# Ten transposes of a pair moved from TensorE to 32x32 VectorE turns with DMA block moves, x loaded transposed as well, and s_dst broadcast by DMA

## The chip, the cores and the metric

The kernel runs on one core of one Trainium2 chip. The metric is device time of one execution in microseconds (us), median over several executions. TensorE is called PE here, its weight loads PEld, VectorE DVE, ScalarE ACT, GpSimd POOL, and SP is the engine whose queue issues the DMAs.

## The reference, cut to what matters

x is (64, 256, 128) in fp32: 64 batches of 256 nodes with 128 features; `adj` is 256x256. Four graph layers follow each other, each added to its input and normalized per row:

```python
x = _layernorm(x + L0(x, adj, ...))   # gated recurrent cell, five steps
x = _layernorm(x + L1(x, adj, ...))   # two weights, softmax of a fixed adjacency
x = _layernorm(x + L2(x, adj, ...))   # attention over nodes, then a small MLP
x = _layernorm(x + L3(x, adj, ...))   # Chebyshev, seven weights
```

The attention of L2 is where one part of the change lies:

```python
h = einsum('bmi,ih->bmh', x, Wp) + bp
s_src = einsum('bmh,h->bm', h, a_src)
s_dst = einsum('bmh,h->bm', h, a_dst)
scores = s_src[:, :, None] + s_dst[:, None, :]      # s_dst is needed along the free axis, on every row
scores = where(scores >= 0, scores, 0.2 * scores)
attn = softmax(where(A <= 0, min, scores)) * A
h_gat = einsum('bmn,bnh->bmh', attn, h)
```

## The kernel before

The kernel works on 32 pairs of batches; a tile of a pair is 128 partitions x 512 fp32 (four blocks of 128 columns). The operations of all pairs are put into one list by a planner in the kernel (`Schedule`): it knows for each operation its engine or engines and a duration, and for each engine how long its result takes to be seen by others (`SEEN`, 2.5 us for a DMA issued by SP). The list that comes out is emitted in the order of the planned starts. In the traces an engine takes its queue in the order of the built list: in the kernel after, all 3510 DVE records stand in that order, and so do, line by line, those of ACT and PE's matmuls.

```python
CLASSES = {"X": (512, 12), "A": (512, 34), "H": (516, 5), "B": (1024, 9), "S": (32, 64), "PS": (512, 8)}
SEEN = {"PE": 0.3, "ACT": 0.15, "DVE": 0.15, "POOL": 0.2, "SP": 2.5}
ABREAST = 4
...
    def transposes(i, x_like):
        t = Value("PS", name="ps")
        def fn():
            for c in range(4):
                nc.tensor.transpose(t.at(4, P)[:, c, :], x_like(i)[:, c, :], ident.ap)
        pe(0.46, fn, [i, ident], [t])
        return t

    def spread(i, right):                     # adjacency times a tile: the tile is the stationary operand
        ...
                    nc.tensor.matmul(t.at(2, N)[:, b, :], tokens(i)[:, 2 * b + j, :], right.ap[:, j, :], ...)

    def layer_norm(y, o):
        s, mv, rs = stats(y)                  # bn_stats on DVE, power -0.5 on POOL
        def fn():
            for c in range(4):
                nc.vector.tensor_scalar(tokens(o)[:, c, :], tokens(y)[:, c, :], mv()[:, c, 0:1], rs()[:, c:c + 1],
                                        op0=ALU.subtract, op1=ALU.mult)
        dve(1.4, fn, [y, s], [o])

    def layer2(x2):
        xT = to_sbuf(transposes(x2, tokens), "xT")
        ...                                   # h = x Wp + bp, with s_src as one more column
        sd, u, s = Value("PS", name="ps"), Value("B", name="u"), Value("S", name="nm")
        pe(mm(512), lambda: nc.tensor.matmul(sd.at(512), vdst.ap, xT.at(512), start=True, stop=True), [vdst, xT], [sd])
        for b in range(2):
            dve(0.68, lambda b=b: nc.vector.tensor_add(u.at(4, N)[:, 2 * b:2 * b + 2, :],
                    sd.at(512)[:, None, b * N:(b + 1) * N].to_broadcast([P, 2, N]), maskb.ap), [sd, maskb], [u])
        ...
```

`vdst` is a matrix whose columns are all Wp a_dst, so one matmul gives s_dst on every partition at once.

## Time and profile before

| | before |
|---|---|
| time, median of 3 | 1831.45 us (1829.76 to 1832.07) |
| PE busy, middle 1340 us | 1310 us |
| PE idle, summed over the table of waits | 81 us |

PE is what the time is made of: whatever takes a microsecond of PE work away may shorten the run, and whatever makes PE wait may lengthen it. The lines that carry this are in the prediction.

### The profile page before, as it was taken

The page shows a single profiled execution, that of the slowest core. Times are in us where ns is not written, and L with a number is a line of the kernel's source. Part 1 is how long each engine was busy: PE and PEld are TensorE (multiplying, and loading weights), DVE is VectorE, ACT ScalarE, POOL GpSimd, SP SyncE. Part 2 cuts the span into 40 slices and gives each one's busy share as a digit, 9 for nine tenths or more (in the row PEclk, how much of TensorE's full clock was granted, in tenths as well). Part 3 has the DMA queues.
Part 4 walks back from the last instruction along what each step waited for, and adds up shares of the span by engine and source line. Part 5 has one row for each costly group of instructions (what it writes and reads, how often), then busy time and mean ns, then how long its engine had stood idle before and what let it go on. Part 6 is the DMA issues. An engine that isn't in the chain of part 4 may idle for free. (4 is left out here: it accounts for less than half of the span.)

```text
span 1832.3 us, 22228 instructions
## 1 busy us (share of the span) xinstructions
PE 1741.1 (95%) x7856; PEld 1230.3 (67%) x7856; DVE 1194.5 (65%) x3536; ACT 793.5 (43%) x1586; POOL 438.8 (24%) x519
## 2 busy tenths in 40 slices
PE   8999999999999999999999999999999999998767
PEld 6567576767767667676776666666766667665566
DVE  5466666667767667667776577665667666665753
ACT  3444445444445454434444444444444444443322
POOL 0022212312231221222222212231123222111152
PEclk9999999999999999999999999999999999999778
DMA  4000000000000000000000000000000000000000
GB/s 119 1 1 12 12 12 1 12 12 13 7 12 7 18 6 7 12 13 11 8 13 12 13 12 1 12 12 7 7 0 7 6 7 7 6 1 6 1 1 24
DMA packets 35024, 20.50 MB, mean 11 GB/s; under 512 B 1248, under 2 KB 34528, under 8 KB 34912
## 3 DMA queue, kind: packets, MB, share of 16 engines
q1 hardware_dynamic: 34912, 19.08, 3.6%
q8 instruction: 61, 1.00, 0.2%
q14 instruction: 51, 0.42, 0.1%
HBM read 10.69 MB, written 8.39 MB: 10 GB/s over the span
## 5 line engine op out<-in xcount | busy, mean ns | idle before, releaser
L173 ACT COPY a<-ps 128x512 f32<-128x512 f32 (+1 forms) x532 | 278.5, 541 | 483.5 <-PE ps L400 286.0
L419 POOL TENSOR_SCALAR s<-s 128x4 f32<-128x4 f32 x160 | 49.5, 310 | 986.1 <-DVE s L416 986.1
L400 PE MATMUL ps<-aT,a 128*128 128x256 f32 x1024 | 242.8, 379 | 1.7 <-ACT a L173 1.6
L400 PEld LDWEIGHTS ps<-aT,a 128*128 128x128 f32 x1024 | 189.9, 190 | 49.5 <-issue 24.5
L422 POOL TENSOR_TENSOR s<-s,neg_half 128x4 f32<-128x4 f32 x192 | 200.4, 1044 | 15.9
L430 DVE TENSOR_SCALAR x<-a,s 128x128 f32<-128x128 f32 x384 | 120.9, 370 | 100.1 <-POOL s L422 99.9
L462 DVE TENSOR_TENSOR a<-a,a 128x512 f32<-128x512 f32 x160 | 121.0, 756 | 95.4 <-ACT a L460 95.2
L460 ACT ACTIVATE a<-ps,bzrh 128x512 f32<-128x512 f32 x160 | 109.9, 687 | 160.6 <-PE ps L458 160.5
L446 ACT ACTIVATE a<-ps,bzrh 128x512 f32<-128x512 f32 x160 | 109.4, 685 | 160.1 <-PE ps L443 156.8
L448 DVE SCALAR_TENSOR_TENSOR a<-a,a 128x512 f32<-128x512 f32 x160 | 120.9, 759 | 81.1 <-ACT a L446 80.5
L414 DVE BATCH_NORM_STATS2 s<-a 128x6 f32<-128x128 f32 x640 | 141.5, 279 | 47.9 <-ACT a L173 45.7
L450 PE MATMUL ps<-a,w 128*128 128x512 f32 x320 | 163.0, 600 | 7.2 <-ACT a L446 7.0
L458 PE MATMUL ps<-a,u5h 128*128 128x512 f32 x320 | 164.4, 595 | 4.9 <-DVE a L448 4.9
L443 PE MATMUL ps<-a,w 128*128 128x512 f32 x320 | 163.6, 593 | 1.8 <-ACT a L173 1.8
L457 PE MATMUL ps<-a,w 128*128 128x512 f32 x320 | 164.5, 596 | 0.0
L442 PE MATMUL ps<-a,W 128*128 128x512 f32 x320 | 163.9, 594 | 0.0
L481 PEld LDWEIGHTS ps<-W,a 128*128 128x128 f32 x1024 | 131.7, 196 | 36.6 <-issue 17.9
L481 PE MATMUL ps<-W,a 128*128 128x128 f32 x1024 | 135.6, 281 | 8.7 <-DVE a L488 4.4
L452 ACT ACTIVATE a<-ps,bzrh 128x512 f32<-128x512 f32 x160 | 110.0, 688 | 62.7 <-PE ps L450 61.3
L400 PE MATMUL ps<-aT,x 128*128 128x256 f32 x512 | 129.3, 391 | 8.1 <-DVE x L430 7.7
L463 DVE SCALAR_TENSOR_TENSOR a<-a,a 128x512 f32<-128x512 f32 x160 | 118.5, 745 | 16.3 <-ACT a L452 13.9
L382 PEld LDWEIGHTS ps<-ident,a 128*128 128x128 f32 x768 | 92.4, 142 | 53.3 <-issue 23.2
(140 smaller groups left out, 2645.6 us busy)
## 6 DMA issues: line engine op xcount, KB each, us to landing
x<-x_in SPq DMA_DIRECT2D x32, 256.0 KB, 2.8
y_out<-a SPq DMA_DIRECT2D x32, 256.0 KB, 2.3
W<-mats_in SPq DMA_DIRECT2D x1, 832.0 KB, 6.7
W<-mats_in SPq DMA_DIRECT2D x1, 512.0 KB, 3.7
rbc<-rows_in SPq DMA_DIRECT2D x1, 385.0 KB, 7.2
aT<-adjT_in SPq DMA_DIRECT2D x1, 256.0 KB, 4.7
a<-adj_in SPq DMA_DIRECT2D x1, 256.0 KB, 5.9
ccol<-cols_in SPq DMA_DIRECT2D x1, 6.0 KB, 3.5
```

Source lines behind the costliest of these rows:

```text
L173: S.add([("ACT", us_act, lambda: nc.scalar.copy(o(), i())), ("DVE", us_dve, lambda: nc.vector.tensor_copy(o(), i()))], r, w)
L400: nc.tensor.matmul(t.at(2, N)[:, b, :], tokens(i)[:, 2 * b + j, :], right.ap[:, j, :], start=(j == 0), stop=(j == 1))
L414: nc.vector.bn_stats(st.at(4, 6)[:, c, :], tokens(y)[:, c, :])
L422: pool(1.04, lambda: nc.gpsimd.tensor_tensor(rs(), rs(), neg_half.ap, op=ALU.pow), [s, neg_half], [s])
L430: nc.vector.tensor_scalar(tokens(o)[:, c, :], tokens(y)[:, c, :], mv()[:, c, 0:1], rs()[:, c:c + 1], op0=ALU.subtract, op1=ALU.mult)
L442: nc.tensor.matmul(t.at(512), mat("u3"), hT.at(512), start=True, stop=False)
L443: nc.tensor.matmul(t.at(512), w345.ap[:, 1, :], mT.at(512), start=False, stop=True)
L450: pe(mm(512), lambda t=t, mT=mT: nc.tensor.matmul(t.at(512), w345.ap[:, 0, :], mT.at(512), start=False, stop=True, skip_group_check=True), ...
L457: nc.tensor.matmul(t.at(512), w345.ap[:, 2, :], mT.at(512), start=True, stop=False)
L458: nc.tensor.matmul(t.at(512), u5h.ap, r.at(512), start=False, stop=True)
L462: dve(0.7, lambda hv=hv, hT=hT: nc.vector.tensor_sub(hv.at(512), hv.at(512), hT.at(512)), [hv, hT], [hv])
L481: nc.tensor.matmul(tokens(t)[:, c, :], i.at(4, P)[:, c, :], w(), start=(k == 0), stop=(k == len(lefts) - 1))
```

## The change

The intent is to take PE work away. (1) Ten of the twelve calls of `transposes` in a pair (four blocks each) become "turns"; two of the ten make up one tile of 1024 columns, so there are nine turns: DVE transposes each 32x32 block in place of its tile, one DMA stores the tile in DRAM, and four DMAs load it so that the blocks are where they belong. A turned tile is interleaved: the 128 columns of block t are every fourth column (every eighth in the 1024-wide tile, wT). (2) x is given a second time, transposed, so that layer 0 needs no transpose for its start. (3) s_dst comes as one more column of h; a DMA stores that column to DRAM ("the line") and a second one loads it onto all 128 partitions. (4) The normalization is split: DVE makes the product -mean*rstd, then ACT or DVE scales. In the attention of L2 the product with the adjacency moves in front of the turn, to POOL or DVE. (5) Buffers, `ABREAST` and the order of a few additions follow from that; the last three pairs keep their turns on PE.

```diff
+ABREAST = 2
+BY_PE = 3
+    def tile(self, t, n=512):
+        return self.ap[:, t:n:n // P] if self.moved else self.ap[:, t * P:(t + 1) * P]
 ...
+    def turn(i, name, o=None, n=512):
+        ...                                  # the last BY_PE pairs: transposes on PE, as before
+        st = Value(cls, name="turn")
+        dve(n / 512 * 0.62 + 0.06, lambda: nc.vector.transpose(st.at(n).rearrange("p (b l t) -> p t b l", b=4, l=32),
+                                                               i.at(n).rearrange("p (t b l) -> p t b l", b=4, l=32)), [i], [st])
+        d = Value("D", name="turn")
+        S.add([("SP", 0.45, lambda: nc.sync.dma_start(d.at(n), st.at(n)))], [st], [d])
+        def move():
+            for f in range(4):
+                nc.sync.dma_start(o.at(n)[32 * f:32 * f + 32].rearrange("r (b n) -> r b n", b=4),
+                                  d.at(n)[:, f * n // 4:(f + 1) * n // 4].rearrange("(b r) n -> r b n", b=4))
+        S.add([("SP", 1.8, move)], [d], [o])
+        o.moved = True
 ...
-                    nc.tensor.matmul(t.at(2, N)[:, b, :], tokens(i)[:, 2 * b + j, :], right.ap[:, j, :],
+                    nc.tensor.matmul(t.at(2, N)[:, b, :], i.tile(2 * b + j), right.ap[:, j, :],
 ...
+        nmr = lambda: s.at(32)[:, 12:16]
+        dve(0.16, lambda: nc.vector.scalar_tensor_tensor(nmr(), mv()[:, :, 0], -1.0, rs(), op0=ALU.mult, op1=ALU.mult), [s], [s])
+    def normalize(y, o, s, rs, nmr):
+        ...                                  # y * rs + nmr
+        S.add([("ACT", 1.85, by_act), ("DVE", 1.45, by_dve)], [y, s], [o])
 ...
-        pe(mm(512), lambda: nc.tensor.matmul(sd.at(512), vdst.ap, xT.at(512), start=True, stop=True), [vdst, xT], [sd])
+        line = lambda *ap: bass.AP(tensor=d.ap.tensor, offset=d.ap.offset, ap=ap)
+        S.add([("SP", 0.45, lambda: nc.sync.dma_start(line([1, P], [P, 4]), hs()[:, :, D + 1]))], [h], [d])
+        S.add([("SP", 0.45, lambda: nc.sync.dma_start(sd.at(512), line([0, P], [1, 512])))], [d], [sd])
```

(The same replacement of `transposes` by `turn` and of block indexing by `tile` is made in all layers; the cuts are marked by "...".)

## The prediction

> **What bounds the kernel now.** I read the head of the page and its 40 slices first, then the busy time by stretch, then TensorE's own timeline in the middle of the run, and last the groups of instructions and the DMA rows. The head and the slices:
>
> ```profile
> span 1832.3 us, 22228 instructions
> PE 1741.1 (95%) x7856; PEld 1230.3 (67%) x7856; DVE 1194.5 (65%) x3536; ACT 793.5 (43%) x1586; POOL 438.8 (24%) x519
> PE   8999999999999999999999999999999999998767
> PEclk9999999999999999999999999999999999999778
> ```
>
> TensorE is busy in nearly every slice until the last three, where its clock falls too. No other engine is above 65%. The table of stretches says how close to full it is:
>
> ```profile
> 0.00:60.00 60.00, 53.67 (x200) 35.18 (x201) 33.46 (x86) 21.76 (x36) 0.83 (x7) 1.00 0.32 91
> 60.00:1400.00 1340.00, 1310.30 (x5934) 920.44 (x5933) 897.58 (x2603) 603.20 (x1201) 326.30 (x380) 1.00 0.03 9
> 1700.00:1832.00 132.00, 91.45 (x482) 77.69 (x480) 73.06 (x295) 38.99 (x101) 40.62 (x52) 0.80 0.03 9
> ```
>
> In the long middle PE (first busy column) works 1310 of 1340 us. The tail of 132 us has only 91 us of PE work at a clock of 0.80. So this is a TensorE-bound kernel with a latency-bound tail. Matmul durations overlap, so I price PE by the distance between starts:
>
> ```profile
> 902.29 0.60 PE L382 MATMUL ps<-ident,x 128*128 128x128 f32 x4
> 902.73 1.89 PE L400 MATMUL ps<-aT,a 128*128 128x256 f32 x8
> 904.46 1.02 PE L457 MATMUL ps<-a,w 128*128 128x512 f32 x2
> 905.32 1.02 PE L458 MATMUL ps<-a,u5h 128*128 128x512 f32 x2
> 906.17 1.50 PE L481 MATMUL ps<-W,a 128*128 128x128 f32 x12
> 907.51 0.60 PE L382 MATMUL ps<-ident,a 128*128 128x128 f32 x4
> ```
>
> Four transposes take 0.44 us (0.11 each), eight 256-column records 1.73 us (0.216 each), two 512-column records 0.86 us (0.43 each), twelve 128-column records 1.34 us (0.112 each). An fp32 matmul shows as two records, a transpose as one. The groups that the change touches:
>
> ```profile
> L382 PE MATMUL ps<-ident,a 128*128 128x128 f32 x768 | 114.3, 277 | 13.8 <-DVE a L465 11.5 <-DVE a L430 2.3
> L382 PE MATMUL ps<-ident,x 128*128 128x128 f32 x512 | 77.5, 279 | 2.9 <-DVE x L430 2.9
> L284 PE MATMUL ps<-ident,b 128*128 128x128 f32 x256 | 37.2, 285 | 10.6 <-ACT b L529 10.6
> L510 PE MATMUL ps<-a,vdst 128*128 128x512 f32 x64 | 34.2, 616 | 0.0
> L173 ACT COPY a<-ps 128x512 f32<-128x512 f32 x418 | 236.0, 587 | 364.2 <-PE ps L400 286.0 <-PE ps L382 69.2 <-DVE a L564 3.0
> x<-x_in SPq DMA_DIRECT2D x32, 256.0 KB, 2.8
> y_out<-a SPq DMA_DIRECT2D x32, 256.0 KB, 2.3
> 178.00 0.39 SPq L602 DMA_DIRECT2D y_out<-a  x1
> ```
>
> [...] the trace's one undisturbed 512-column add from SBUF (line 305) took 692 ns, so I use it, as an estimate, for the block turns. [...] the two whole 256 KB trips in the trace take 2.3 us (store) and 2.8 us (load). [...]
>
> **The change part by part.** Counts come from the built instruction lists of both kernels.
>
> *PE, removed.* Transposes fall from 1544 to 256: 44 of the 48 of a pair in 29 of 32 pairs (the last three keep theirs, except the four of the first x), 29 x 44 + 3 x 4 = 1288. At 0.11 us that is 141.7 us. The 32 s_dst matmuls are 64 records at 0.43 = 27.5 us. Together 169 us, and all of it lies on the engine that sets the pace. Check of the whole: before, 1664 x 0.43 + 2832 x 0.216 + 1536 x 0.112 + 256 x 0.1125 + 1544 x 0.11 = 1698 us of PE pace; the other 134 us of the span are start, small gaps, tail and slow clock. After: 1529 us.
>
> *DVE.* Added: 232 turns of 512 columns x 0.69 + 29 turns of 1024 x 1.22 [...] = 195 us; 160 small scale products x 0.16 = 26 us. Removed: PSUM copies 62 to 15 (47 x 0.687 = 32 us); normalizations 640 to 292 because ACT may take them now (348 x 0.36 = 125 us); the products with aT 64 to 10 (54 x 0.684 = 37 us). Net +27: 1195 becomes about 1222 us, not the bound.
>
> *ACT.* Copies 418 to 270 (-148 x 0.587 = -87), normalizations 128 to 476 (+348 x 0.465 = +162): about 868 us. *POOL* gains 54 products of 128x512, 1.35 us each from its similar rows (1.30 to 1.44): +73, about 512 us. Neither binds.
>
> *SP and DMA.* 64 DMAs of the loop become about 1465: 261 stores to DRAM, 4 x 261 loads, 64 for s_dst, 96 for x, its transpose and y. At 0.39 us plus a gap of 0.07 between issues each takes 0.46, so 674 us: SP is some 40% occupied. Bytes: 29 x (8 x 0.5 + 1 MB) = 145 MB plus loads, about 95 GB/s, where the existing 19 MB took 3.6% of the 16 DMA engines. The 512-byte pieces of a turn are like those of an x load. Scaled by bytes, 28%, maybe 40% with the many small pieces: room enough.
>
> *Latency.* One turn now takes 0.69 (DVE) + 2.3 (store) + three further issues 1.4 + 2.3 to 2.8 (last load) = about 7 us, against 0.44 + 0.59 (transpose and ACT copy). That is +6 us for each of nine turns, and +4 for s_dst (2.3 + 2.8 against 0.86): nearly 60 us per pair. The first result left at 178 us, so a pair lives some 170 us and about 3.3 pairs overlap at 52 us of PE work each. After: 230 us and 47 us, five pairs. Twelve x tiles and 36 A tiles should allow that, so most of the latency hides behind other pairs. It comes out at the start and wherever the fixed order of an engine queue, above all the one SP queue, runs late; I charge 25 us more idle PE.
>
> *Sum.* 1529 + 134 + 25 = about 1690 us, if a weight load from a moved tile costs what a dense one costs.
>
> **Rivals.**
>
> *Strided weight loads.* A moved tile is read as every fourth fp32[...]. Such tiles are the stationary operand of 48 records of 256 columns and 32 of 128 columns per pair (wpx 8, the attention product 16, zT 8). [...] Against it: the changed kernel's scheduler prices these matmuls as before, in a kernel otherwise carefully priced.
>
> *DMA latency becomes the wait.* With one in-order issuer, each store must land before its four loads are issued; if turns of different pairs hardly overlapped, 9 x 4.5 us (store 2.3, issues 1.8, gaps) + s_dst 5 = 46 us per pair, which is just PE's 47. Then PE would wait everywhere and the time would be 1800 to 1900. For it: one queue. Against it: the built list interleaves stores of two or three pairs before loads.
>
> *VectorE becomes the bound.* If the turns' strided writes ran at half rate, +29 x (8 x 0.53 + 1.07) = 154 us: DVE 1376, still below 1690, but its queue would delay others: 1720 to 1750.
>
> *Tail.* The scheduler now ranks all but the last two pairs by age instead of the last four; the tail may grow by 10 to 20 us. Keeping the last pairs on PE speaks against more.
>
> **Range and chances.** I weigh the plain case (about 1690) at 0.5, half-rate weight loads (about 1780) at 0.33, stalls of DMA or DVE (1750 to 1900) at 0.17. The middle of that is 1712 us; eight times in ten between 1650 and 1800. Faster by over 2% means below 1795: 0.80; within 2%: 0.12; slower: 0.08.
>
> **What would show it.** Right: PE busy near 1560 us, above 90% of the middle slices, transposes 256, DVE near 1220, a store landing in about 2.3 us. Half-rate weight loads: weight-load records of moved tiles well above 190 ns and starts of the attention product 0.2 us apart instead of 0.112. DMA stalls: PE idle before the matmuls that read moved tiles, released by DMA, over 100 us in sum. DVE: turns well above 0.69 us, and PE waiting for DVE. The prediction is wrong if moved tiles are read slower than half rate, or if the SP queue runs so late that PE drops below 85% in the middle.

## More of the kernel before

The framework that builds the kernel can still order the emitted instructions a second time, which matters later (e16, e17).

One more group is needed later, for comparison: the weight loads of two matmuls whose stationary operand the change will lay out differently. The columns are line, engine, operation, tiles, shape and count, then the busy sum and mean ns of one, then idle time.

```profile
L400 PEld LDWEIGHTS ps<-aT,a 128*128 128x128 f32 x1024 | 189.9, 190 | 49.5 <-issue 24.5 <-ACT a L173 4.1 <-ACT a L460 0.5
...
L543 PEld LDWEIGHTS ps<-h,b 128*128 128x128 f32 x512 | 63.2, 195 | 8.6 <-issue 5.1 <-DVE b L535 2.2 <-DVE x L430 0.2
```

Both load 128x128 in about 0.19 us, beside running matmuls.

## The result, and the profile after

The changed kernel takes 2097.54 us (2096.17 to 2100.61, 4 runs) against 1831.03 us for the kernel before in the same rounds; the ratio is 1.1458, with a 95% interval of 1.1438 to 1.1478. It is correct and clearly slower. (All ratios here are the mean time of one kernel's fast runs over the mean of the other's fast runs of the same rounds, so they are not quite the ratio of the medians quoted.) The prediction was 1712 us, with 1800 as the upper end of its range.

The head of the page and the slices of PE and its clock, after:

```profile
span 2094.4 us, 22712 instructions
...
PE 1785.4 (85%) x6504; PEld 1273.9 (61%) x6504; DVE 1360.7 (65%) x3510; ACT 845.6 (40%) x1784; POOL 509.1 (24%) x573
...
PE   8998798888987889988788788987989888967846
...
PEclk9999999999998999999999899999999999978978
```

PE executes 1352 records fewer than before (6504 against 7856) and yet is busy 44 us longer, and in most slices it is busy for only seven or eight tenths. So two things happened: what is left on PE is slower, and PE waits. No other engine is near its limit. The summed idle time before PE's records rose from 81 to 301 us. The stretch in the middle says the same (PE is the first busy column, the clock and the DMA share are the two fractions near the end):

```profile
60.00:1400.00 1340.00, 1177.17 (x4147) 824.79 (x4146) 902.19 (x2197) 542.95 (x1112) 310.50 (x341) 0.95 0.37 98
```

Where before 1310 of these 1340 us were PE work, it is now 1177. The DMA engines are busy 0.37 of the time, so they are not full. How long the new DMAs take, from issue to landing in us (last column):

```profile
d<-a SPq DMA_DIRECT2D x232, 256.0 KB, 2.1
a<-d SPq DMA_DIRECT2D x928, 64.0 KB, 2.1
...
a<-d SPq DMA_DIRECT2D x32, 256.0 KB, 4.9
...
d<-h SPq DMA_DIRECT2D x32, 2.0 KB, 9.3
```

The first two rows are the turns, and they are as quick as I had assumed. The last two are the line: the store of 2 KB takes 9.3 us, over four times as long as the store of 256 KB, and its broadcast 4.9 us. Two waits answer to it (us in total, times, longest), one in the table of the engines' waits and one in that of the DMA queue:

```profile
DVE b L567 <- DMA a<-d: 171.3, 26, 14.2
```

```profile
SPq L565 <- DMA d<-h: 199.3, 28, 11.6
```

DVE stands for 171 us in sum at the addition that reads the line, up to 14.2 us at a time. One such place in the timeline:

```profile
893.60 0.76 DVE L559 TENSOR_TENSOR h<-ps,hbias 128x260 f32<-128x260 f32 x2
...
894.38 0.38 SPq L564 DMA_DIRECT2D d<-h  x1
...
904.19 0.34 SPq L565 DMA_DIRECT2D a<-d  x1
...
908.22 0.69 DVE L567 TENSOR_TENSOR b<-a,maskb 128x512 f32<-128x512 f32 x1 [8.93 <-DMA a<-d]
908.83 0.68 DVE L545 TENSOR_TENSOR a<-ps,a 128x512 f32<-128x512 f32 x1
...
909.57 1.11 PE L398 MATMUL ps<-ident,x 128*128 128x128 f32 x4 [4.48 <-DVE a L545]
...
910.47 1.92 PE L511 MATMUL ps<-a,w 128*128 128x512 f32 x2
...
912.18 1.91 PE L512 MATMUL ps<-a,u5h 128*128 128x512 f32 x2
```

The column of h is ready at 894.4; the store needs until 904.2, the load until 908.2. DVE idles 8.93 us at L567. L545, which has nothing to do with the line and belongs to another pair, stands behind it in DVE's queue, and PE waits 4.48 us for L545. Then PE's two-record matmul starts 1.71 us before the next (910.47 to 912.18), where before the change it was 0.86: after these 4.48 us of idle time it runs at half pace. The trace shows the clock granted to PE: it is 1.00 in the stretch from 893 to 906 us, 0.50 from 908.2 to 914 us, and 1.00 again from 915 us.

The other loss shows in the groups. These three answer to the two weight-load groups of before and to the estimate of 0.69 us for a turn:

```profile
L447 PEld LDWEIGHTS ps<-aT,a 128*128 128x128 f32 x1024 | 256.4, 315 | 65.8 <-issue 33.5 <-DMA a<-d 8.6 <-DVE s L463 5.4
...
L422 DVE STREAM_TRANSPOSE a<-a 128x512 f32<-128x512 f32 x174 | 190.8, 1107 | 9.3 <-ACT a L482 5.2 <-PE ps L637 1.4 <-PE ps L447 0.4
...
L598 PEld LDWEIGHTS ps<-h,b 128*128 128x128 f32 x512 | 122.0, 326 | 15.1 <-issue 11.5 <-ACT b L188 0.9 <-DMA t<-xT_in 0.2
```

A weight load from an interleaved tile takes 0.32 us on the mean instead of 0.19, the last pairs' dense ones included, and a turn of 512 columns takes 1.107 us.

### The profile page after: what moved, and what is told of

It reads as the page before. It is cut to its first block, busy times and chain, and to the rows that moved or that the text cites. A ratio compares the mean times of both kernels' runs of the same rounds, so it can differ in the third digit from the quotient of the medians.

```text
span 2094.4 us, 22712 instructions
## 1 busy us (share of the span) xinstructions
PE 1785.4 (85%) x6504; PEld 1273.9 (61%) x6504; DVE 1360.7 (65%) x3510; ACT 845.6 (40%) x1784; POOL 509.1 (24%) x573
## 2 busy tenths in 40 slices
DMA packets 253164, 189.50 MB, mean 90 GB/s; under 512 B 40048, under 2 KB 215152, under 8 KB 253040
## 5 line engine op out<-in xcount | busy, mean ns | idle before, releaser
L188 ACT COPY a<-ps 128x512 f32<-128x512 f32 (+1 forms) x379 | 194.5, 518 | 368.5 <-PE ps L447 214.3
L447 PEld LDWEIGHTS ps<-aT,a 128*128 128x128 f32 x1024 | 256.4, 315 | 65.8 <-issue 33.5
L447 PE MATMUL ps<-aT,a 128*128 128x256 f32 x1024 | 274.3, 410 | 17.4 <-DMA a<-d 16.7
L533 PEld LDWEIGHTS ps<-W,a 128*128 128x128 f32 x1024 | 159.8, 228 | 64.4 <-ACT a L188 21.0
L422 DVE STREAM_TRANSPOSE a<-a 128x512 f32<-128x512 f32 x174 | 190.8, 1107 | 9.3 <-ACT a L482 5.2
L533 PE MATMUL ps<-W,a 128*128 128x128 f32 x1024 | 166.4, 311 | 34.2 <-ACT a L188 10.9
L471 DVE SCALAR_TENSOR_TENSOR s<-s 128x4 f32<-128x4 f32 x192 | 45.3, 236 | 173.4 <-POOL s L469 173.0
L567 DVE TENSOR_TENSOR b<-a,maskb 128x512 f32<-128x512 f32 x64 | 43.0, 706 | 171.3 <-DMA a<-d 171.3
L512 PEld LDWEIGHTS ps<-a,u5h 128*128 128x128 f32 x320 | 60.7, 198 | 136.5 <-DVE a L502 77.2
L482 ACT ACTIVATE x<-a,s 128x128 f32<-128x128 f32 x212 | 90.5, 485 | 116.1 <-DVE s L471 116.0
```

The source lines that it names most:

```text
L188: S.add([("ACT", us_act, lambda: nc.scalar.copy(o(), i())), ("DVE", us_dve, lambda: nc.vector.tensor_copy(o(), i()))], r, w)
L422: dve(n / 512 * 0.62 + 0.06, lambda: nc.vector.transpose(st.at(n).rearrange("p (b l t) -> p t b l", b=4, l=32), i.at(n).rearrange("p (t b ...
L447: nc.tensor.matmul(t.at(2, N)[:, b, :], i.tile(2 * b + j), right.ap[:, j, :], start=(j == 0), stop=(j == 1))
L482: nc.scalar.activation(tokens(o)[:, c, :], tokens(y)[:, c, :], AF.Identity, bias=nmr()[:, c:c + 1], scale=rs()[:, c:c + 1])
L512: nc.tensor.matmul(t.at(512), u5h.ap, r.at(512), start=False, stop=True)
L533: nc.tensor.matmul(tokens(t)[:, c, :], i.tile(c), w(), start=(k == 0), stop=(k == len(lefts) - 1))
```

## The experiments

The first theory was: the line through DRAM costs most, because in-order queues stand behind it; the interleaving costs about 100 us; the turns' own trips are mostly hidden. The rivals: what PE waits for is the turns' trips through the one SP queue, or the interleaving is the main loss. The theory of the line had to be changed once on the way (e5, e16). "before" in the ratios is the kernel before in the same rounds, 1831 to 1832 us.

| label | what runs | us | ratio to before |
|---|---|---|---|
| (after) | the whole change | 2097.54 | 1.1458 |
| e1_sdst_pe | s_dst on PE | 1935.95 | 1.0573 |
| e2_dense_weights | moved tiles read dense (wrong results) | 2062.1 | 1.126 |
| e3_dense_turn_writes | turns written dense (wrong results) | 2047.57 | 1.1174 |
| e4_turns_by_pe | turns on PE | 2119.12 | 1.1573 |
| e5_line_planned | the plan knows the line's latency | 2090.53 | 1.1415 |
| e6_sdst_pe_dense_both | e1 with e2 and e3 (wrong results) | 1825.44 | 0.997 |
| e7_turns_sdst_by_pe | e1 with e4 | 1872.28 | 1.0225 |
| e8_turns_sdst_by_pe_ab4 | e7 with ABREAST = 4 | 1882.47 | 1.028 |
| e9_line_16B | the line stored in 16-byte pieces | 1989.62 | 1.0871 |
| e10_before_strided | kernel before, weights read interleaved (wrong results) | 1944.0 | 1.0613 |
| e11_before_xT | kernel before, x loaded transposed as well | 1829.92 | 0.9991 |
| e12_turns_sdst_norm_by_pe | e7, normalization as before | 1837.58 | 1.0029 |
| e13_turns_few | e12 with the turns of layers 0 and 3 | 1827.3 | 0.9975 |
| e14_turns_only_dense | e12 with all turns, dense (wrong results) | 1803.71 | 0.9847 |
| e15_turns_only | e12 with all turns | 1898.74 | 1.0366 |
| e16_line_planned_turns_by_pe | e4 with e5 | 2145.23 | 1.1715 |
| e17_line_planned_turns_by_pe_held | e16, built order held to the plan | 1778.29 | 0.9715 |
| e18_line_planned_held | e5, built order held to the plan | 1922.06 | 1.0499 |

"Wrong results": the data come out in the wrong order, while every instruction, its size and its waits stay.

**e1_sdst_pe: s_dst back on PE.**

```diff
-        S.add([("SP", 0.45, lambda: nc.sync.dma_start(line([1, P], [P, 4]), hs()[:, :, D + 1]))], [h], [d])
-        S.add([("SP", 0.45, lambda: nc.sync.dma_start(sd.at(512), line([0, P], [1, 512])))], [d], [sd])
+        def scores():
+            for c in range(4):
+                nc.tensor.matmul(sd.at(4, P)[:, c, :], vdst.ap, xT.tile(c), start=True, stop=True)
+        pe(mm(512), scores, [vdst, xT], [sd])
```

> Only the s_dst part undone: a TensorE matmul broadcasts s_dst again (four 128-column matmuls), the turns stay. Theory LINE (the 4-byte-piece store of s_dst takes 9.3 us, its load 4.9 us, the in-order SP and DVE queues stand behind it, and TensorE then restarts at half clock): DVE's 171 us of waiting on it go, the time falls by 170 us or more, to about 1900, although PE work grows by about 30 us. Theory WEIGHTS (slow loads of strided stationary tiles are nearly all of the loss): the time stays near 2080 to 2110. Theory TURN LATENCY (the trip of a turn through DRAM is what stalls PE): also near 2080.

Measured: 1935.95 us, 162 us below the kernel after. The line costs that much, although its removal gives PE work back. That work is itself slower than before, because the moving operand xT is interleaved here: the 256 records are 393 ns long on the mean, against 278 ns in e6, where xT is read dense, and they start 0.216 us apart on the mean instead of 0.114. That is some 26 us of PE work (256 x 0.102) which e1 and e15 have and the real change doesn't, since there s_dst is not PE's. The line is the largest single loss but not the whole of it.

**e2_dense_weights and e3_dense_turn_writes: the interleaving alone, at one end each.**

```diff
 e2: -        return self.ap[:, t:n:n // P] if self.moved else self.ap[:, t * P:(t + 1) * P]
     +        return self.ap[:, t * P:(t + 1) * P]
 e3: -  nc.vector.transpose(st.at(n).rearrange("p (b l t) -> p t b l", b=4, l=32), ...
     +  nc.vector.transpose(st.at(n).rearrange("p (b t l) -> p t b l", b=4, l=32), ...
```

> Wrong results on purpose: TensorE reads each moved tile as 128 neighbouring columns instead of every fourth; all else and the order of instructions are the same. WEIGHTS: from the records of the changed kernel, 29 pairs x (32 records x (0.230-0.112) + 48 x (0.247-0.216)) = 153 us of PE pace go; the time falls to about 1945. LINE or TURN LATENCY: PE has 15% idle and waits for others, so less than half of it shows, 2030 or more. Weight-load records of the attention product should fall from a mean of 326 ns to about 195.

> Wrong results on purpose: VectorE writes the turned blocks in runs of 32 neighbouring columns instead of every fourth; DMA and TensorE are unchanged. A turn of 512 columns should fall from 1107 to about 690 ns, 121 us of DVE work in all. If VectorE's work is on the path the time falls by 60 to 120 us, to about 2000; if it lies beside other work (DVE is 65% busy) by less than 40, to 2060 or more.

Measured: 2062.1 and 2047.57 us, 35 and 50 us below the kernel after. The mechanism shows in the records: with dense reads the weight loads of the attention product fall to 217 ns and PE's busy time from 1785 to 1695 us; with dense writes a turn takes 700 ns instead of 1107. But PE saved 90 us of busy time in e2 and only 35 us of the run: PE was waiting, and finished its work sooner only to wait longer (its summed idle time rises from 301 to 358 us). In e3 DVE saves 95 us and the run 50, which lies between the two forecasts: DVE's slow turns are partly on the path. In a kernel that stands still elsewhere, taking away one cost underrates it.

**e4_turns_by_pe and e7_turns_sdst_by_pe: no turns by DVE at all, with and without the line.**

```diff
-BY_PE = 3
+BY_PE = 32
```

> All ten turns of every pair on TensorE as in the last three pairs; s_dst still goes through DRAM, x still comes transposed. PE pace 1529 + 29 x 44 x 0.11 = 1669 us with no strided weights, no DVE turns and no DMA trips but that of s_dst. LINE: the stall of s_dst stays, and the time is 1900 to 2000, slower than the kernel before. WEIGHTS or TURN LATENCY: the time is near the kernel before less its saved transposes of x, about 1800 to 1830.

> Turns and s_dst on TensorE; left of the change are x loaded transposed, the normalization on either engine, the product with the adjacency before the transpose, the scheduler's two abreast. LINE: PE pace 1698 - 14 (transposes of x) = 1684 us, + 134 = about 1818, so some 300 us below the run with turns on TensorE and s_dst through DRAM, and a shade faster than before. If that run's loss came from the other small changes instead, it stays above 2000.

Measured: 2119.12 us with the line and 1872.28 without. Both forecasts for e4 missed: it is slower than either theory had it. With not one turn going through DRAM the kernel is no faster, which speaks against the turns' trips as what stalls the kernel after, and the line alone accounts for 247 us between the two. The comparison is not clean, since in e4 the wait at the line is longer than the 171.3 us of the kernel after:

```profile
DVE b L567 <- DMA a<-d: 257.7, 31, 18.5
```

But e7 is not back at 1832 us either, with turns and s_dst both on PE. Something else of the change costs about 40 us. (A more direct sign against the turns' trips: in the kernel after, PE's waits for the turns' loads sum to 37 us, where the prediction asked for over 100.)

**e8_turns_sdst_by_pe_ab4 and e12_turns_sdst_norm_by_pe: what is left in e7.** e8 sets `ABREAST = 4` as before; e12 gives the normalization back its old form (layer 2's first one, on ACT with the product, was so before):

```diff
     def layer_norm(y, o):
-        normalize(y, o, *stats(y))
+        s, mv, rs = stats(y)
+        dve(1.4, fn, [y, s], [o])            # tensor_scalar: subtract mean, multiply by rstd
```

> As the previous run but with the scheduler's last four pairs abreast again, as in the kernel before. If two abreast costs in the tail, 5 to 20 us faster than the previous run, about 1805; if not, the same within 5 us.

> Turns and s_dst on TensorE, and the normalization as in the kernel before (no scale product that sends the result from POOL through VectorE, only one engine allowed). If the way the normalization is split costs the 40 us that its parent lost against the kernel before: about 1825 to 1840. If the order of product and transpose, the tiles or the two abreast cost them: the same as the parent, 1872 within 8.

Measured: 1882.47 us, 10 us worse than e7, so ABREAST is not it; and 1837.58 us, 35 us better. The split normalization costs what was missing, with the order as built. Why it does is only argued. DVE waits for POOL's power about as long in both forms: 219.9 us in sum before its product in e7 (L474), 201.8 us before its normalizations and the one product that is left in e12. New in e7 is a further hop: where ACT scales, it waits for DVE's product, 130.8 us in sum against 71.4 us in e12. PE does not wait for that itself; what it waits for most in e7 is DVE's update in layer 0 (L522, 33.9 us), which may come late behind the products. No run takes the hop alone.

**e6_sdst_pe_dense_both: no line and no interleaving.** The edits of e1, e2 and e3 together.

> Wrong results on purpose: s_dst by TensorE, dense weight reads and dense turn writes together; what is left of the change are the DRAM trips of the turns. If the trips hide, as the prediction had it: 1529 + 28 us of PE pace + 134 + some 25 us of small gaps = about 1720, a gain over before. If TURN LATENCY stalls PE: 1800 or more. From the run with s_dst on TensorE at 1936, WEIGHTS alone should now give back its 153 us plus about 30 for the strided moving operand of the s_dst matmuls.

Measured: 1825.44 us, in the band of the rival (1800 or more) and not at 1720. Part of the gap is the split normalization (35 us), part is waiting that the turns bring after all (in e14, below, PE waits about 60 us more than without them). Against e1 (1935.95) the interleaving costs 111 us once the line no longer hides it, some 26 of them for the s_dst operand; e2 and e3 had shown 35 and 50. And against e7 (1872.28) it shows what turns without interleaving would win: 47 us.

**e10_before_strided: the interleaved weight loads on the kernel before.** The stationary operand of the same matmuls is read as every fourth column (wT: every eighth), in a kernel without turns, line or added DMAs:

```diff
+    def pick(v, t, n=512):
+        return v.ap[:, t:n:n // P] if v.name in ("h", "xT", "zT", "wT") else v.ap[:, t * P:(t + 1) * P]
```

> Wrong results on purpose: the kernel before with its turned tiles (h, xT, zT, wT) read by TensorE at every fourth column, nothing else. WEIGHTS on a TensorE that does not wait: 32 pairs x (32 x 0.118 + 48 x 0.031) = 169 us, to about 2000. If the loss from strided loads is smaller than the records suggest: under 1950. Note that the dense-weight run of the changed kernel won only 35 us.

Measured: 1944.0 us, 112 us above the kernel before, with PE busy 97% of the span. This is the clean measurement of the disputed cost, less than the 169 us that I had worked out. Three things make the difference. There are 40 records of 256 columns with such an operand in a pair and not 48 (32 in layer 0, 8 in layer 3). They start 0.240 us apart on the mean in this trace and not 0.247. And PE's summed idle time falls from 81 to 54 us, so part of the cost fills time in which PE had waited. Summed over the groups of this trace against the kernel before, the spacing costs 143 us; less the 27 us of idle time that is 116. The weight load is as slow as in the kernel after:

```profile
L546 PEld LDWEIGHTS ps<-h,b 128*128 128x128 f32 x512 | 125.4, 335 | 7.3 <-issue 3.0 <-DVE b L538 2.2 <-DVE x L433 0.2
```

335 ns against 195. (b is wT, so this is the load of every eighth column; the loads of every fourth take 318 to 327 ns on the mean against 190 to 194.) The attention product's records start 0.234 us apart on the mean instead of 0.114.

**e11_before_xT: only x loaded transposed, on the kernel before.**

> The kernel before with one part of the change: x is also loaded transposed from DRAM, three tiles in rotation. It takes 4 x 32 transposes (14 us of PE pace) and 32 copies off: about 1815, 0.5 to 1% faster than before. If the three tiles hold back the start of pairs, it is 1840 or more, and explains the 40 us that the run with turns and s_dst on TensorE lost.

Measured: 1829.92 us, ratio 0.9991 with an interval of 0.9979 to 1.0004. It takes 128 transposes away, 14 us of PE pace, and wins nothing that can be told from zero; both forecasts missed.

**e9_line_16B: the line in 16-byte pieces.** DVE first packs the column to 128x4; the store then moves 128 pieces of 16 bytes instead of 512 pieces of 4 bytes, and the addition reads every fourth column.

```diff
-        S.add([("SP", 0.45, lambda: nc.sync.dma_start(line([1, P], [P, 4]), hs()[:, :, D + 1]))], [h], [d])
+        dve(0.16, lambda: nc.vector.tensor_copy(sc.at(4), hs()[:, :, D + 1]), [h], [sc])
+        S.add([("SP", 0.45, lambda: nc.sync.dma_start(line([4, P], [1, 4]), sc.at(4)))], [sc], [d])
```

> The changed kernel; VectorE first copies the four s_dst columns side by side, so that the store has 128 pieces of 16 bytes instead of 512 of 4 bytes; VectorE then reads the broadcast line at every fourth column. If the number of small pieces makes the store slow: it lands in 3 to 4 us instead of 9.3, some 6 us per pair less, and the time falls by 80 to 170 us, to 1930 to 2020. If small stores to DRAM are slow however many pieces: no change, 2080 or more.

Measured: 1989.62 us, 108 us below the kernel after. The store lands in 1.4 us:

```profile
d<-s SPq DMA_DIRECT2D x32, 2.0 KB, 1.4
```

Cutting the line into 4-byte pieces made the store slow (on its reading or its writing side: e9 packs both). The number of pieces is not enough to explain it: the store of y_out has 512 pieces too, of 512 bytes each, and lands in 2.3 us in the kernel before. Nor is it the sending: in the trace of e17 the 512 packets of 4 bytes have all started 1.2 us after the issue, and the completion comes at 8.9 us. Why it comes so late was not looked into. The packets show the splitting: with 128 pieces in place of 512 in each of 32 stores, the packets under 512 bytes fall by 32 x 384, from 40048 to 27760.

**e5_line_planned and e16_line_planned_turns_by_pe: tell the planner.** The planner is given 9.3 and 4.9 us for the two DMAs of the line in place of 2.5 us, in the kernel after (e5) and with turns on PE (e16).

```diff
-        S.add([("SP", 0.45, lambda: nc.sync.dma_start(line([1, P], [P, 4]), hs()[:, :, D + 1]))], [h], [d])
-        S.add([("SP", 0.45, lambda: nc.sync.dma_start(sd.at(512), line([0, P], [1, 512])))], [d], [sd])
+        S.add([("SP", 0.45, lambda: nc.sync.dma_start(line([1, P], [P, 4]), hs()[:, :, D + 1]))], [h], [d], 9.3)
+        S.add([("SP", 0.45, lambda: nc.sync.dma_start(sd.at(512), line([0, P], [1, 512])))], [d], [sd], 4.9)
```

> The changed kernel with all its operations; only the scheduler is told that the store of s_dst lands 9.3 us and its load 4.9 us after the issue, instead of 2.5 us each, so that it puts other work of the SP and VectorE queues in front of what waits for them. LINE as a fault of the fixed order (queues stand behind a late transfer): the 171 us of VectorE waiting shrink below 60, the time falls to about 1900 to 1960, near the run with s_dst on TensorE. LINE as sheer latency of the pair's chain (order does not matter): within 40 us of the changed kernel, about 2060 to 2100.

> Correct results. As e4 (turns on TensorE, s_dst line by DMA through DRAM, 2119 us), but the order of the instructions is planned with 9.3 and 4.9 us for the line's two DMAs instead of 2.5 us each. Theory (a queue whose order is fixed with too short a latency stands still behind the line): with the order right, most of the 247 us between e4 and e7 comes back, 1880 to 1950 us. Rival (the latency itself, with too few pairs in flight): within 30 us of e4, 2090 us or more.

Measured: 2090.53 us, 7 us below the kernel after, and 2145.23 us, 26 us worse than e4. My theory of a plan with too short a latency fell, as it stood. (In e5 DVE's wait for the line did fall, from 171.3 to 107.1 us and not below 60, and PE's wait for a turn's load at L448 rose to 50.3 us from 16.7.) But the trace of e16 does not look like its plan. Here is the line of the first pair, on DVE: the column of h is complete at 119.5, and the addition with the line is at 132.31.

```profile
119.09 0.42 DVE L560 TENSOR_TENSOR h<-ps,hbias 128x260 f32<-128x260 f32 x1
...
124.05 0.85 DVE L478 TENSOR_SCALAR x<-a,s 128x128 f32<-128x128 f32 x3
132.31 1.29 DVE L568 TENSOR_TENSOR b<-a,maskb 128x512 f32<-128x512 f32 x2 [7.40 <-DMA a<-d]
```

Right after L478, DVE comes to L568 and stands 7.40 us. The plan of the kernel has eight more DVE operations of other pairs between the two. They are not there: the framework that builds the kernel orders the emitted instructions a second time. Over all lines, the built list of e16 has a median of 6 DVE operations between the column and the addition, just as in e4; a list in the order of the plan has 18. (A run of like instructions counts as one here; counted singly in the traces, it is 9 in e16 and 30 in e17.) In the trace DVE worked 3.6 us of the 13.1 us that the line takes (mean of 27 lines between 100 and 1800 us), and waited 7.9 at the addition.

**e17_line_planned_turns_by_pe_held: the built order held to the plan.** Nothing but this is added to e16:

```diff
     for op, fn in S.order(tiles):
         ...
         fn()
+        for i in made[n:]:                   # the instructions that fn() emitted
+            if i.engine in ahead:
+                tc.add_manual_dep(i, ahead[i.engine].name, mybir.DependencyInfo(
+                    mybir.DependencyClass.NoSync, mybir.DependencyReason.DATA), reason="in the planned order")
+            ahead[i.engine] = i
```

> Correct results. e16 (turns on TensorE, s_dst line by DMA, planned with the measured 9.3 and 4.9 us; 2145 us) with one more thing: on each engine an instruction may not be issued ahead of the one that the kernel's own plan puts before it, so that the build no longer moves the sum with the line forward. The built list now has a median of 18 VectorE instructions between the column and that sum, against 6 in e16. Theory (VectorE's queue comes to the line too early, stands there, and TensorE starves behind it): VectorE's wait for the line falls from 255 us to below 60, and the time to 1830 to 1900 us. Rival (the latency as such, or the plan's own errors, cost the time): above 2050 us, or the waits only move to other instructions.

Measured: 1778.29 us, better than forecast: 367 us below e16 and 2.85% below the kernel before (interval 2.68 to 3.01%), correct. The same wait in e16 and in e17:

```profile
DVE b L568 <- DMA a<-d: 255.0, 31, 15.6
```

```profile
DVE b L568 <- DMA a<-d: 16.4, 3, 12.1
```

And the same line of the first pair in e17, with fourteen rows between the column and the addition:

```profile
120.12 0.42 DVE L560 TENSOR_TENSOR h<-ps,hbias 128x260 f32<-128x260 f32 x1
...
135.09 0.68 DVE L546 TENSOR_TENSOR a<-ps,a 128x512 f32<-128x512 f32 x1
135.69 1.28 DVE L568 TENSOR_TENSOR b<-a,maskb 128x512 f32<-128x512 f32 x2
```

The addition comes later than in e16 and nobody waits for it. The line still takes its 13 us (its store 8.9 us, its load 4.5). With turns on PE it is thus not the latency as such that is lost, but the place of its reader in an in-order queue. The line of the engines on the page of e17:

```profile
PE 1688.0 (95%) x7664; PEld 1205.5 (68%) x7664; DVE 1221.5 (69%) x3507; ACT 904.2 (51%) x1820; POOL 525.8 (30%) x569
```

PE is at 95% again and idles 78 us in sum, against 343 in e16. The gain of 367 us is more than the line's 247 (e4 less e7), so holding the order must have repaired more than the line. In sum it is 265 us of PE's idle time and 102 us of its busy time (1790.0 us in e16), for the same 7664 records: the granted clock is 0.981 in place of 0.926. Which places gained, was not looked into. A run of the kernel before with its order held would have told how much of the 2.85% belongs to the change and how much to the order; it was not made, and this stays open. It may in part be the order: e17 has the line and the split normalization and is still 59 us faster than e12, which has neither; and built again, the kernel before is reordered too (at 425 places among its 3536 DVE instructions one follows another that was emitted after it; in e16 at 538 of 3507, in e17 at none).

**e18_line_planned_held: the whole change, line planned, order held.**

> Correct results. The kernel after with the line's measured latency in the plan (e5, 2090 us) and the built order held to the plan, turns by VectorE and DMA. Theory: the line's cost goes as in e17, what stays is the stride (about 111 us) and the split normalization (35 us) less what the turns win: 1880 to 1950 us. Rival (the turns' own trips, planned at 2.5 us for each SP instruction, need the rearrangement by the build): no better than e5, 2050 us or more.

Measured: 1922.06 us, 168 us below e5. The line has left the list here too. What PE waits for most are now the turns' loads:

```profile
PE ps L448 <- DMA a<-d: 33.5, 8, 8.5
PE ps L599 <- DMA b<-d: 25.6, 8, 7.0
PE ps L637 <- DMA a<-d: 24.1, 6, 6.0
```

With the order held, turning on DVE makes the kernel 144 us slower than turning on PE (e17). The turns' DMAs are still planned at 2.5 us each; whether a better plan hides them was not tried.

**e13, e14, e15: the turns alone.** The line and the split normalization are both taken out (as e12), the order is the build's, and the turns are in three forms: six of the nine turns (e13: layers 0 and 3), all of them dense (e14, wrong results), all of them as in the change (e15).

```diff
 e13: -        xT = turn(x2, "xT")
      +        xT = turn(x2, "xT", far=False)         # on PE; wT and zT of layer 2 likewise
```

> Correct results. s_dst on TensorE and the normalization as before; only the four turns of layer 0 and the one of layer 3 go by VectorE and DMA, the other three (one of them 1024 wide) are TensorE's. Theory (the turns trade TensorE work for strided weight loads): they take away 20 x 0.11 = 2.2 us of transposes per pair, 29 pairs: 64 us, and make 32 records of 256 columns start 0.247 us instead of 0.216 us apart (29 us), so some 35 us below e12 (1837.6): 1800 us. Rival (what the turns win is given back as waits for their DMA trips in an in-order queue): 1840 to 1870 us.

> Wrong results on purpose: turns write, and moved tiles are read, as dense runs of columns. s_dst on TensorE and the normalization as before, every turn by VectorE and DMA. If the three costs add up (line, stride, split normalization), this is e6 (1825.4) less the 35 us of the normalization, 1790 us. Rival (the waits of the turns' trips take it up): no better than 1820 us.

> Correct results. The turns in their real, strided form, s_dst on TensorE and the normalization as before. If the costs add up: e1 (1936) less 35 us, 1900 us; the strided moving operand of s_dst adds some 30 us to that already. Rival (the split normalization costs only where the turns are TensorE's and VectorE is what the chain waits for): 1935 us, as e1.

Measured: 1827.3, 1803.71 and 1898.74 us, beside 1837.58 with no turn (e12). Without the interleaving the turns win 34 us; the interleaving takes 95 us; in their real form they lose 61, of which some 26 are the interleaved s_dst operand. e15 is as forecast if the costs add up; e14 lies between its two forecasts. PE's busy time falls from 1734 (e12) to 1640 us (e14), that is 94 us, and PE's summed idle time rises from 92 to 152 us: about 60 of the 94 us come back as waiting. e13 misses its expectation of 1800 us (which counted five turns where there are six, so it should have been lower still); at 0.9975 of before (interval 0.9959 to 0.9992) it is a gain of 0.25%, clear of noise but too small to build on.

One form could not be built: a layout in which the moved tile keeps dense 32-column runs needs a stationary operand with two free dimensions, and the build refuses that with the message that it must have exactly one.

## Why the prediction was wrong, point by point

The runs telescope from before to after, with the order as built in all of them, each step one difference of medians: e12 less before +6 us (transposed x, buffers, ABREAST); e15 less e12 +61 us (turns as they are); e1 less e15 +37 us (split normalization); after less e1 +162 us (the line). The sum is +266, as measured. The prediction had -119 in their place (1712 against 1831). (The 1712 is not the mean of its own cases: with 1825 for the stalls, 0.5 x 1690 + 0.33 x 1780 + 0.17 x 1825 is 1743.) The line is the largest failed step and not the only one: without it (e1) the kernel is still 5.7% slower than before.

1. **The line: the step that failed.** The prediction put "+4 for s_dst (2.3 + 2.8 against 0.86)" and charged 25 us of PE idle for all latencies together. The store takes 9.3 us and not 2.3: I took the latency of a 256 KB transfer for a transfer of 512 single elements, and bytes were the wrong thing to go by (e9: 16-byte pieces in place of 4-byte ones, 1.4 us). The trip is about 14 us, and it stands in front of an in-order engine: 162 us in the whole change, 247 us with the turns on PE.

2. **"Most of the latency hides behind other pairs": the wrong test.** I argued that five pairs in flight give enough other work. With the turns on PE they do: e17 hides the same 13 us trip behind 10.6 us of DVE work and waits 0.5 us on the mean, and e18, the whole change, waits only 10.7 us in sum. But DVE used the other work only where its queue had that work ahead of the waiting instruction (it waited 255.0 us for the line in e16, 16.4 in e17). The built list, not the number of pairs, decides this, and it was there to be counted before the run: in the changed kernel it has a median of 10 DVE operations between the column and the addition, about 7 us of work in the trace, against a trip of 14. The prediction did look at the built list, but only for the turns' stores and loads.

3. **The half-rate weight loads: the mechanism was right, its probability and one size were not.** The prediction gave it a third and about 1780 us, 90 above its plain case; how much of a slower weight load shows in the spacing of the records was an estimate of mine, which the trace of the kernel before did not show. The plain case, to which it gave a half, rested on "if a weight load from a moved tile costs what a dense one costs", and that step failed. The records of 128 columns went from 0.112 to 0.23 us, where the rival said 0.2; those of 256 columns went from 0.216 to 0.24. Their count is 40 a pair and not 48. With the spacings first read in the trace, 29 x (32 x 0.118 + 40 x 0.031) = 146 us; measured in isolation, 112 us on the kernel before (e10), 95 to 111 us with turns (e15 less e14, e1 less e6; these two include the turns' slower writes and the interleaved s_dst operand). So it costs more than the removal of the transposes wins.

4. **DVE's turns.** Put at 0.69 us, measured 1.107; with dense writes 0.700 (e3), so the 692 ns of the add at line 305 were right for the instruction and the interleaved write is the difference. (The 1.22 us for 1024 columns, and the 0.53 us by which the rival lengthened a turn of 512, are estimates; in the trace before, DVE instructions of 128, 512 and 1024 columns take 284, 692 and 1209 ns at lines 370, 305 and 518, which is 0.52 to 0.54 us for each further 512 columns. A turn of 1024 took 2036 ns, and 1238 with dense writes.) The total of DVE, 1361 us, is near the 1376 of that rival. It did not become the bound, but it delayed others, as that rival had it (30 to 60 us more): dense writes win 50 us in e3.

5. **The removed PE work.** The counts held: 1352 records fewer is what 1288 transposes and 64 s_dst records make. The worth did not: of 94 us that leave PE with dense turns, 34 reach the time. The charge of 25 us for latency should have been about 60 for the turns alone.

6. **Not in the prediction at all: the split normalization.** It was counted as work moved from DVE to ACT. It costs 35 us (e7 less e12); that it does so as a chain with one more hop is argued, not shown.

7. **The DMA rival.** It named one SP queue that is late with the turns. By the prediction's own sign, over 100 us of PE waiting for loads of moved tiles, it fails: 37 us in the kernel after. Turns by PE did not help either (e4). So this is not the main loss; but the trips are not free (point 5), and they come to the fore when the order is held (e18).

It is thus not enough that other work exists: it has to be ahead of the reader in the reader's queue. That is shown by e16 and e17, which have the same counts of instructions on every engine, in a different order. What is only argued is why the build moves the reader forward; its reasons were not looked at.

## What to carry to other kernels

Before trusting that a latency is hidden, count in the built instruction list how much work stands between the producer and the consumer on the consumer's engine, and compare it with the measured trip; a plan made in the kernel may be undone by the build, and holding it was worth 367 us here. Do not estimate a small DMA by its bytes: 2 KB in pieces of 4 bytes took 9.3 us, four times as long as 256 KB in pieces of 512 bytes (2.3 us). A layout that saves a transpose must be priced at every later read of it, above all where it is loaded as a matmul's weights (318 to 335 ns a load in e10 against 190 to 195), and a cost that shows little in a kernel that waits elsewhere must be measured in one that doesn't.
